# A Fourier token mixer in a four-layer network: its 32-point transforms on halves of the TensorE array, its last transform and projection by thirds of the channels

## The chip, the cores and the metric

The kernel runs on one core of one Trainium2 chip. The metric is the device time of one execution in microseconds (us). Before the change the median of three runs is 3758.2 us (3753.52 to 3759.49). One profiled execution, from which all durations below come, took 3750.98 us.

## The reference, cut to what matters

The network has four layers on an image batch of B = 4, C = 96 channels and 64 x 64 = 4096 tokens, all in float32. Layers 0 to 2 and the last feed-forward part are not touched. The change is in the first half of layer 3, which mixes tokens by a Fourier transform with H = 192 hidden channels:

```
h = relu(bn1(einsum('bnc,hc->bnh', x, w1)))
X = fft(h, axis=1, norm='ortho')
xr = relu(X.real * rd - X.imag * idg + rb)
xi = relu(X.imag * rd + X.real * idg + ib)
y = ifft(xr + 1j * xi, axis=1, norm='ortho').real
o = bn2(einsum('bnh,ch->bnc', y, w2))
t = t + o
```

Here x is the layer-normed t, and rd and idg are the diagonals of two matrices.

## The kernel before, in words

The 4096-point transform is split as 4096 = 128 x 32: a transform over 128 points, a multiplication by twiddle factors, and a transform over 32 points; the inverse goes back the same way. The 192 channels of an image are handled in groups of four, so 48 groups. A 128 x 128 matrix then holds 32 points times 4 channels in its partitions.

`fourier` runs a software pipeline of 32 iterations plus four to drain. Each iteration j starts a new set of G = 6 groups; an image takes eight iterations. The functions, with the lines of their instructions in the profile, are:

- `norm1`, `norm2` (L1306 to L1317): layer norm of the next image's tokens, in the first four iterations of each image but the last.
- `w1` (L1326, L1328): the first projection of the next image, in the other four. ScalarE writes its relu into `hh`.
- `over_n1(j)` (L1340, L1344, L1352): the 128-point transform on TensorE into `s1_ps`; VectorE multiplies it by the twiddles into `p0` and `p1`; GpSimd adds these crosswise into `f` (two instructions of 128 x 390).
- `over_n2(j-1)` (L1361 to L1364, L1367, L1376, L1379, L1380): the 32-point transform, four matmuls of 128 x 128 weights on 390 columns, into `xi_ps` and `xr_ps`; VectorE makes `ec`, ScalarE makes `av` in twelve instructions, and GpSimd adds and subtracts `ec`.
- `fold(j-2)` (L1386, L1391, L1394, L1397): a relu on ScalarE, four VectorE instructions that make `zz` and `z`, and a negation on ScalarE.
- `over_k2(j-3)` (L1409 to L1411): the inverse 32-point transform, twelve matmuls of 128 x 128 weights on 128 columns into two PSUM banks `i1`, copied by ScalarE into `bt`.
- `row64` (L1419 to L1424): the 65th row of `bt`, for which two small transfers go through DRAM.
- `over_k1` (L1444, L1446): the inverse 128-point transform for four tokens n and 96 channels (a "block"); its matrix `gt` is loaded per block by a transfer of 256 KB into one of two buffers; ScalarE copies the result to `ys`.
- `w2` (L1455, L1459, L1461): the second projection of that block, in a `misc` bank of PSUM; VectorE adds it to `t`.

A unit is half of an image's channels (96), so eight units of eight blocks, two blocks per iteration. All engines' orders are written out by hand (`manual_schedule`): each engine executes its instructions in the order of the calls. That order, within an iteration, is over_n1, norm1 or w1, fold, over_k1 of the first block, norm2, over_n2, norm1, w2 of the first block, over_k1 of the second block, over_k2, norm2 or row64 or w1, w2 of the second block. [...] `misc` two, `s1` two, `xr` and `xi` one each, `i1` two.

Of the kernel before, what the change touches and what calls it, by code (L numbers as in the profile page):

```python
# [102 lines left out]
class Net:  # L103
# [717 lines left out]
    def consts2(self, wk, small):  # L821
# [74 lines left out]
        self.a_w2 = pool.tile([C, 2, C], F32, name="a_w2s")  # L896
        for half in range(2):
            ps = small(C, C)
            nc.tensor.matmul(ps, raw[:, half * C : (half + 1) * C], gain, start=True, stop=True)
            nc.vector.tensor_copy(self.a_w2[:, half], ps)  # L900
        self.dft1 = load("dft1", [N1, 2 * 65])
        self.twid = load("twid", [128, 2, 2 * 65])
        self.dft2 = load("dft2", [128, 3 * 128])
# [381 lines left out]
    def fourier(self, dram, t, h):  # L1285
# [3 lines left out]
        units = [(b, half) for b in range(B) for half in range(2)]  # L1289
        its = [(u, g) for u in range(len(units)) for g in range(0, CG, G)]  # L1290
        with ExitStack() as ctx:
# [3 lines left out]
            nbs, bc, bs = (self.dft2[:, k * 128 : (k + 1) * 128] for k in range(3))  # L1295
# [23 lines left out]
            def w1(b, n):  # L1319

                if n == 0:
                    for half in range(2):
                        hh[2 * b + half] = wk.tile([N1, CG, N2, 4], F32, name="hh", tag="hh", bufs=3)
                ps = misc(N1)[:, : 4 * C].rearrange("p (n c) -> p n c", n=2)
                for d in range(2):
                    nc.tensor.matmul(ps[:, d, :], h[:, n + d :: N2], self.a_w1, start=True, stop=True)  # L1326
                for half in range(2):
                    nc.scalar.activation(  # L1328
                        hh[2 * b + half][:, :, n : n + 2, :].rearrange("p g n c -> p n g c"),
                        ps[:, :, half * C : (half + 1) * C].rearrange("p n (g c) -> p n g c", c=4),  # L1330
                        AF.Relu,
                    )

            def over_n1(i):

                u, g = its[i]
                ps = pln.tile([128, 2, MB], F32, name="s1_ps", tag="s1")
                for d in range(G):
                    a = d % 3 * 2 * K1
                    nc.tensor.matmul(ps[:, d // 3, a : a + 2 * K1], hh[u][:, g + d], self.dft1, start=True, stop=True)  # L1340
# [10 lines left out]
                for r in range(2):  # L1351
                    nc.gpsimd.tensor_add(f[i][:, r], pp[0][:, :, r, :], pp[1][:, :, 1 - r, :])  # L1352

            def over_n2(i):

                u, g = its[i]
                cg = units[u][1] * CG + g
                fr, fi = (f[i][:, r].rearrange("p g k -> p (g k)") for r in range(2))
                f.pop(i)
                xr, xi = (pln.tile([128, MB], F32, name=f"x{r}_ps", tag=f"x{r}")[:, : G * K1] for r in "ri")  # L1360
                nc.tensor.matmul(xi, bc, fi, start=True, stop=False)  # L1361
                nc.tensor.matmul(xi, nbs, fr, start=False, stop=True)
                nc.tensor.matmul(xr, bc, fr, start=True, stop=False)
                nc.tensor.matmul(xr, bs, fi, start=False, stop=True)  # L1364
# [17 lines left out]
            def fold(i):  # L1382

                u, g = its[i]
# [3 lines left out]
                if g == 0:  # L1388
                    z64[u] = wk.tile([128, 2, CG], F32, name="z64", tag="z64", bufs=2)
                for k, (one, two, op) in enumerate(((0, 2, ALU.add), (3, 1, ALU.subtract))):  # L1390
# [4 lines left out]
                        z64[u][:, k, g : g + G], v[:, one, :, K1 - 1], 0.0, v[:, two, :, K1 - 1], ALU.max, op  # L1395
# [3 lines left out]
            def over_k2(i):  # L1399

                u, g = its[i]
                z = zz.pop(i)
                if g == 0:
                    bt[u] = wk.tile([N1, N2, C], F32, name="bt", tag="bt", bufs=2)
                for e in range(0, G, 3):
                    ps = pln.tile([N1, 4, 128], F32, name="i1_ps", tag="i1", bufs=2)[:, :3]
                    for d in range(3):
                        zd = z[:, e + d].rearrange("p k m -> p (k m)")
                        nc.tensor.matmul(ps[:, d], zd[:, 64:], bc, start=True, stop=False)  # L1409
                        nc.tensor.matmul(ps[:, d], zd[:, :128], bs, start=False, stop=True)  # L1410
                    nc.scalar.copy(  # L1411
                        bt[u].rearrange("p n (g c) -> p g n c", c=4)[:, g + e : g + e + 3],
                        ps.rearrange("p g (n c) -> p g n c", c=4),
                    )

            def row64(u):
                ps = misc(CG)[:, :128]
                for k in range(2):
                    nc.tensor.matmul(ps, z64[u][:, k], self.dft64[:, k], start=k == 0, stop=k == 1)  # L1419
                r = wk.tile([CG, N2, 4], F32, name="r64", tag="r64", bufs=2)  # L1420
                nc.scalar.copy(r, ps.rearrange("p (n c) -> p n c", c=4))
                d = dram.tile([1, N2 * C], F32, name="d64", tag="d64", bufs=2)
# [5 lines left out]
            def fetch(k):  # L1428

                g = wk.tile([N1, CG, N2, 4], F32, name="hh", tag="hh", bufs=3)  # L1430
                g = g.rearrange("p g n c -> p (g n c)")[:, : N2 // 2 * N1].rearrange("p (n a) -> p n a", n=N2 // 2)
# [4 lines left out]
            def over_k1(u, n, kept):  # L1436
                if n in late:
                    gt = late[n]
                else:
                    gt = wk.tile([N1, 4, N1], F32, name="gt", tag="gt", bufs=2)  # L1440
                    nc.sync.dma_start(gt, ins["idft"][:, n : n + 4])
                ps = misc(C).rearrange("p (n a) -> p n a", n=4)
                for d in range(4):
                    nc.tensor.matmul(ps[:, d], bt[u][:, n + d], gt[:, d], start=True, stop=True)  # L1444
                kept[u, n] = wk.tile([C, MB], F32, name="ys", tag="ys", bufs=2)
                nc.scalar.copy(kept[u, n], ps.rearrange("p n a -> p (n a)"))  # L1446

            def w2(u, n, kept):

                b, half = units[u]  # L1450
                if u < len(units) - 1:
                    ps = misc(C)
                else:
                    ps = pln.tile([N1, 4, 128], F32, name="i1_ps", tag="i1", bufs=2)[:C].rearrange("p n a -> p (n a)")
                nc.tensor.matmul(ps, self.a_w2[:, half, :], kept.pop((u, n)), start=True, stop=True)  # L1455
                ps = ps.rearrange("p (n a) -> p n a", n=4)
                td = ft[b][:, n : n + 4]
                if half == 0:
                    nc.vector.scalar_tensor_tensor(td, ps, self.b2, td, ALU.add, ALU.add)  # L1459
                else:  # L1460
                    nc.vector.tensor_add(td, td, ps)  # L1461

            engines = {mybir.EngineType.PE, mybir.EngineType.DVE, mybir.EngineType.Activation, mybir.EngineType.Pool}
            with tc.manual_schedule(engines=engines):
# [3 lines left out]
                for j in range(len(its) + 4):  # L1468
                    ub, k = divmod(j - 2 * PER, PER)
                    blocks = [(ub, n) for n in (8 * k, 8 * k + 4)] if 0 <= ub < len(units) else []  # L1470
# [30 lines left out]
                    if blocks:  # L1501
                        w2(*blocks[0], kept)
                        over_k1(*blocks[1], kept)
# [6 lines left out]
                    if (j - 6) % PER == 0 and 0 <= (j - 6) // PER < len(units):  # L1510
                        row64((j - 6) // PER)
                    turn(len(tokens))
                    if blocks:
# [4 lines left out]
                last = [(len(units) - 1, n) for n in range(0, N2, 4)]  # L1518
# [31 lines left out]
def _constants():  # L1550
# [9 lines left out]
    th = 2 * np.pi * np.outer(np.repeat(np.arange(N2), 4), k1) / L  # L1560
# [4 lines left out]
    eye = np.eye(4)  # L1565
    bc, bs = np.kron(np.cos(th), eye), np.kron(np.sin(th), eye)
# [115 lines left out]
```

## Time and profile before

| | us |
|---|---|
| median of three runs | 3758.2 |
| profiled execution, its time | 3750.98 |
| its span, first to last instruction | 3749.2 |
| TensorE busy (share of the span) | 3115.1 (83%) |
| VectorE busy | 2981.6 (80%) |
| ScalarE busy | 2720.5 (73%) |
| GpSimd busy | 2566.7 (68%) |

The Fourier part begins at about 3108 us of the span, where its first `w1` matmul starts, and its last block ends at about 3615 us. The first matmul of `over_n1` in each iteration marks the iterations: image 0 at 3125.6 us, image 1 at 3219.1, image 2 at 3346.2, image 3 at 3470.1; the last four of an image start at 3183.9, 3281.2, 3406.9 and 3517.4 us. For images 1 and 2, an iteration is 14.7 to 16.0 us long in most cases; for image 3, where no next image is prepared, 11.6 to 12.3 us. The page's busy shares are means over the whole network; for this change one reads the rows inside 3108 to 3615 us.

In the rows, PE is TensorE's matmul, PEld its weight load, DVE VectorE, ACT ScalarE, POOL GpSimd and SP the queue that issues transfers. A float32 matmul appears as two records. A row of the timeline gives start and length in us, the engine, the line, the operation, out<-in, the shape (for TensorE: rows*columns of the weights, then the moving operand), the count, and in brackets the idle time before and who ended it.

### The profile page before, as it was taken

The page shows a single profiled execution, that of the slowest core. Times are in us where ns is not written, and L with a number is a line of the kernel's source. Part 1 is how long each engine was busy: PE and PEld are TensorE (multiplying, and loading weights), DVE is VectorE, ACT ScalarE, POOL GpSimd, SP SyncE. Part 2 cuts the span into 40 slices and gives each one's busy share as a digit, 9 for nine tenths or more (in the row PEclk, how much of TensorE's full clock was granted, in tenths as well). Part 3 has the DMA queues.
Part 4 walks back from the last instruction along what each step waited for, and adds up shares of the span by engine and source line. Part 5 has one row for each costly group of instructions (what it writes and reads, how often), then busy time and mean ns, then how long its engine had stood idle before and what let it go on. Part 6 is the DMA issues. An engine that isn't in the chain of part 4 may idle for free. (4 is left out here: it accounts for less than half of the span.)

```text
span 3749.2 us, 46836 instructions
## 1 busy us (share of the span) xinstructions
PE 3115.1 (83%) x15326; PEld 1404.9 (37%) x15326; DVE 2981.6 (80%) x2644; ACT 2720.5 (73%) x5456; POOL 2566.7 (68%) x922
## 2 busy tenths in 40 slices
PE   7887888788878887887888888657799997999888
PEld 3232223223222322232233233147344435676643
DVE  5999999999999999999999999931662493444649
ACT  6887888888888888888888888541345685656557
POOL 1899989898999899989989998811001174434527
PEclk8999899899989998999999899658899999999999
DMA  7656665666565666666665666376000000011001
GB/s 187 156 152 160 166 161 148 165 160 172 145 170 152 173 149 169 157 157 161 166 165 142 172 157 173 91 214 217 1 0 1 1 1 6 24 35 46 24 11 57
DMA packets 171644, 446.63 MB, mean 119 GB/s; under 512 B 48756, under 2 KB 50750, under 8 KB 168064
## 3 DMA queue, kind: packets, MB, share of 16 engines
q1 hardware_dynamic: 171400, 443.64, 45.7%
q8 instruction: 121, 1.98, 0.2%
q14 instruction: 123, 1.01, 0.1%
HBM read 369.97 MB, written 73.50 MB: 118 GB/s over the span
## 5 line engine op out<-in xcount | busy, mean ns | idle before, releaser
L648 POOL TENSOR_TENSOR hs<-hs,crep 128x2048 f32<-128x2048 f32 x384 | 1601.2, 4185 | 224.2 <-DVE hs L643 176.4
L610 ACT ACTIVATE da<-ddb,nega 128x1024 f32<-128x1024 f32 x576 | 661.5, 1149 | 197.7 <-DMA ddb<-dd 124.3
L643 DVE TENSOR_TENSOR_SCAN hs<-da,state,rep 128x1024 f32<-128x1024 f32 x288 | 669.2, 2338 | 39.6 <-PE rep L594 21.9
L621 POOL TENSOR_TENSOR up<-udb,brep 128x1024 f32<-128x1024 f32 x192 | 453.0, 2360 | 73.1 <-DMA udb<-ud 58.9
L665 PE MATMUL y<-hs,sel_r 128*32 128x512 f32 x3072 | 459.6, 692 | 12.8 <-POOL hs L648 12.3
L599 PE MATMUL rep<-dbl,sel_b 32*128 32x512 f32 x768 | 250.1, 730 | 215.1 <-DVE hs L643 215.0
L507 ACT ACTIVATE uta<-delta,bt 128x192 f32<-128x192 f32 x1024 | 381.1, 446 | 0.0
L287 PE MATMUL ps<-n,w_x 97*64 97x512 f32 x1536 | 353.8, 602 | 13.0 <-ACT xc L411 12.1
L643 DVE TENSOR_TENSOR_SCAN hs<-da,state,u 128x1024 f32<-128x1024 f32 x144 | 338.1, 2348 | 23.9 <-PE y L665 8.2
L643 DVE TENSOR_TENSOR_SCAN hs<-dap,state,up 128x1024 f32<-128x1024 f32 x144 | 335.2, 2328 | 0.5 <-ACT dap L610 0.5
L594 PE MATMUL rep<-ident,uta 128*128 128x128 f32 x1536 | 222.6, 287 | 105.6 <-DVE hs L643 93.2
L594 PEld LDWEIGHTS rep<-ident,uta 128*128 128x128 f32 x1536 | 174.9, 146 | 246.5 <-issue 133.3
L636 DVE TENSOR_TENSOR u<-udb,rep 128x1024 f32<-128x1024 f32 x192 | 235.4, 1226 | 24.8 <-DMA udb<-ud 11.4
L1240 POOL CAST hq<-y 128x1536 fp8e5<-128x1536 f16 x64 | 94.0, 1469 | 218.1 <-issue 122.6
L643 DVE TENSOR_TENSOR_SCAN hs<-da,rep 128x1024 f32<-128x1024 f32 x96 | 217.9, 2282 | 21.2 <-PE rep L594 14.8
L610 ACT ACTIVATE dap<-ddb,nega 128x1024 f32<-128x1024 f32 x192 | 214.8, 1119 | 24.9 <-DVE hs L643 24.4
L636 DVE TENSOR_TENSOR rep<-udb,rep 128x1024 f32<-128x1024 f32 x192 | 232.0, 1208 | 0.0
L287 PEld LDWEIGHTS ps<-n,w_x 97*64 97x64 f32 x1536 | 103.8, 137 | 260.2 <-issue 210.0
L665 PEld LDWEIGHTS y<-hs,sel_r 128*32 128x32 f32 x3072 | 73.7, 118 | 335.2 <-issue 257.7
L599 PEld LDWEIGHTS rep<-dbl,sel_b 32*128 32x128 f32 x768 | 65.8, 205 | 353.6 <-issue 295.2
L658 PE MATMUL y<-xc,dp 128*128 128x512 f32 x192 | 125.7, 743 | 31.3 <-ACT bt L463 31.3
L1379 POOL TENSOR_TENSOR av<-av,ec 128x780 f32<-128x780 f32 x32 | 58.8, 1837 | 133.7 <-ACT av L1376 133.7
(275 smaller groups left out, 6201.3 us busy)
## 6 DMA issues: line engine op xcount, KB each, us to landing
udb<-ud SPq DMA_DIRECT2D x768, 128.0 KB
ddb<-dd SPq DMA_DIRECT2D x768, 128.0 KB
crep<-cd SPq DMA_DIRECT2D x512, 128.0 KB
dd<-delta SPq DMA_DIRECT2D x64, 384.0 KB
band<-in_band SPq DMA_DIRECT2D x24, 1024.0 KB
ud<-delta SPq DMA_DIRECT2D x62, 384.0 KB
brep<-cd SPq DMA_DIRECT2D x128, 128.0 KB
x<-in_x SPq DMA_DIRECT2D x32, 384.0 KB
```

Of the source, the lines that this page charges most:

```text
L287: nc.tensor.matmul(ps[rows], w[:, 64 * p : 64 * p + 64], rhs[:, at.start + shift : at.stop + shift], start=k == 0, stop=k == len(ws) - 1, ...
L507: nc.scalar.mul(m["uta"][:, q, :, 32 * s4 : 32 * s4 + 32].rearrange("t (p j) d -> t p j d", p=3), m["udt"][:, :, q].rearrange("t p (j d) - ...
L594: nc.tensor.transpose(x[:, q * 128 : q * 128 + 128], made[k]["uta"][:, q, 2 * h + j], self.ident)
L599: nc.tensor.matmul(x[:, at], sel_b[rows, g], made[k]["dbl"][rows, at], start=True, stop=True)
L610: nc.scalar.activation(da, made[k]["dd", h, j], AF.Exp, scale=nega[:, col : col + 1])
L621: nc.gpsimd.tensor_mul(up, made[k]["ud", p][:, j], made[k]["brep", GP])
L636: nc.vector.tensor_mul(u, made[k]["ud", h][:, j], x)
L643: nc.vector.tensor_tensor_scan(hs[:, 1:], made[k].pop(("da", t)), u, st, ALU.mult, ALU.add)
L648: nc.gpsimd.tensor_mul(hs[:, :, :T], hs[:, :, 1:], twice(made[k]["crep", g]))
L658: nc.tensor.matmul(y, dp[:, items[k][2], p], made[k]["xc"][:, p], start=True, stop=True)
L665: nc.tensor.matmul(made[k]["y", p][row : row + 32], sel_r, made[k]["hs", p, g][:, j, at], start=False, stop=True, skip_group_check=True,)
L1240: nc.gpsimd.tensor_copy(q, y2, saturate=False)
```

## The change

- `over_n2`: the partitions are laid out so that real and imaginary part of two channels lie together. Four matmuls with 128 x 64 weights replace the four with 128 x 128; a pair writes the two halves of the partitions of one bank. To lay `f` out this way GpSimd makes it in four instructions of 64 x 390 instead of two of 128 x 390.
- `over_k2`: 24 matmuls with 64 rows of weights and 64 columns moving replace twelve with 128 and 128. Even and odd ones lie on the two halves of the array's rows and write two banks, `i0` and `i1`. Copies to `bt` go by bank; where a group set crosses a third of the channels there are four instead of two.
- A unit is a third of an image's channels (64), so twelve units. A block of `over_k1` is eight tokens by 64 channels: eight matmuls with 128 x 64 weights in pairs on column halves, two `gt` transfers, and one copy to `ys` of all 128 partitions. There are 48 blocks instead of 64.
- `w2`: a block's projection is two matmuls with 64 x 96 weights on row halves, into the banks `i0` and `i1` instead of a `misc` bank, and two VectorE additions to `t`.
- Schedule: units become ready after iterations 5, 8 and 10 of an image; an iteration takes one or two blocks by the pattern (2, 1, 2, 2, 1, 1, 2, 1).
- `hh`, `twid`, the small constant matrices and the vectors of `rd`, `idg`, `rb`, `ib` are laid out to fit.

```diff
-                for r in range(2):
-                    nc.gpsimd.tensor_add(f[i][:, r], pp[0][:, :, r, :], pp[1][:, :, 1 - r, :])
+                for q, rows in enumerate(parts):
+                    for r in range(2):
+                        nc.gpsimd.tensor_add(f[i][parts[r], q], pp[0][rows, :, r, :], pp[1][rows, :, 1 - r, :])
...
-                nc.tensor.matmul(xi, bc, fi, start=True, stop=False)
-                nc.tensor.matmul(xi, nbs, fr, start=False, stop=True)
-                nc.tensor.matmul(xr, bc, fr, start=True, stop=False)
-                nc.tensor.matmul(xr, bs, fi, start=False, stop=True)
+                for r, x in ((1, xi), (0, xr)):
+                    for q, rows in enumerate(parts):
+                        nc.tensor.matmul(
+                            x[rows], self.dft2[:, r], fs[:, q], start=True, stop=True, skip_group_check=True
+                        )
...
-                for e in range(0, G, 3):
-                    ps = pln.tile([N1, 4, 128], F32, name="i1_ps", tag="i1", bufs=2)[:, :3]
-                    for d in range(3):
-                        zd = z[:, e + d].rearrange("p k m -> p (k m)")
-                        nc.tensor.matmul(ps[:, d], zd[:, 64:], bc, start=True, stop=False)
-                        nc.tensor.matmul(ps[:, d], zd[:, :128], bs, start=False, stop=True)
...
+                ps = [pln.tile([N1, MB], F32, name="i_ps", tag=f"i{q}") for q in range(2)]
+                for d in range(G):
+                    zd = z[:, d].rearrange("p k m -> p (k m)")
+                    for k, m in enumerate((bc, bs)):
+                        for p, rows in zip(ps, parts):
+                            nc.tensor.matmul(
+                                p[:, d * 64 : d * 64 + 64],
+                                zd[rows, 64 - 64 * k : 192 - 64 * k],
+                                m[rows],
...
+                for d in range(4):
+                    for q, rows in enumerate(parts):
+                        nc.tensor.matmul(
+                            ps[rows, d],
+                            bt[u][:, n + 4 * q + d],
+                            gts[q][:, d],
...
-                nc.tensor.matmul(ps, self.a_w2[:, half, :], kept.pop((u, n)), start=True, stop=True)
-                ps = ps.rearrange("p (n a) -> p n a", n=4)
-                td = ft[b][:, n : n + 4]
...
+                ps = [pln.tile([N1, MB], F32, name="i_ps", tag=f"i{q}")[:C] for q in range(2)]
+                for p, rows in zip(ps, parts):
+                    nc.tensor.matmul(p, self.a_w2[rows, third], y[rows], start=True, stop=True)
+                for q, p in enumerate(ps):
+                    p = p.rearrange("p (n a) -> p n a", n=4)
+                    td = ft[b][:, n + 4 * q : n + 4 * q + 4]
...
-                    blocks = [(ub, n) for n in (8 * k, 8 * k + 4)] if 0 <= ub < len(units) else []
+                    todo += [(u, n) for r, u in ready if r + 2 == j for n in range(0, N2, 8)]
+                    many = (2, 1, 2, 2, 1, 1, 2, 1)[j % 8]
+                    blocks, todo = todo[:many], todo[many:]
...
                     if blocks:
                         w2(*blocks[0], kept)
+                    if len(blocks) > 1:
                         over_k1(*blocks[1], kept)
...
                         over_k2(j - 3)
...
-                    if blocks:
+                    if len(blocks) > 1:
                         w2(*blocks[1], kept)
```

## The prediction, before the result was known

> **What bounds the kernel now.** The page first, for the size of things, then the busy times by stretch for the Fourier part: TensorE looks like the bound.
>
> ```profile
> 3346.15:3406.86 60.71, 56.92 (x293) 36.71 (x292) 31.27 (x45) 39.60 (x95) 29.62 (x23) 1.00 0.13 36
> 3406.86:3470.05 63.19, 57.24 (x325) 46.49 (x324) 28.16 (x36) 36.80 (x107) 24.72 (x19) 1.00 0.17 51
> 3470.05:3564.50 94.45, 84.30 (x522) 63.68 (x521) 61.79 (x72) 54.22 (x146) 47.27 (x32) 1.00 0.08 24
> ```
>
> After the length come PE, PEld, DVE, ACT, POOL busy. PE fills about 90%. But a record's end lies about 0.16 us past its columns, so I read one iteration in order of time:
>
> ```profile
> 3517.43 1.50 PE L1340 MATMUL s_ps<-dft,hh 128*128 128x130 f32 x12
> 3517.63 1.25 DVE L1459 SCALAR_TENSOR_TENSOR t<-m_ps,bn_b,t 96x512 f32<-96x512 f32 x1 [3.19 <-PE m_ps L1455]
> 3519.02 1.85 DVE L1344 TENSOR_TENSOR p<-s_ps,twid 128x780 f32<-128x780 f32 x2
> 3519.43 0.85 ACT L1386 ACTIVATE av<-av 128x780 f32<-128x780 f32 x1 [2.19 <-POOL av L1380]
> 3520.79 0.55 DVE L1391 SCALAR_TENSOR_TENSOR zz<-av 128x384 f32<-128x384 f32 x1
> 3521.01 2.44 POOL L1352 TENSOR_TENSOR f<-p,p 128x390 f32<-128x390 f32 x2 [1.61 <-DVE p L1344]
> 3521.25 0.85 DVE L1394 SCALAR_TENSOR_TENSOR z<-av 128x6 f32<-128x6 f32 x1
> 3522.61 0.52 ACT L1397 ACTIVATE zz<-zz 128x384 f32<-128x384 f32 x1 [2.32 <-DVE zz L1391]
> 3523.04 0.56 ACT L1446 COPY ys<-m_ps 96x512 f32<-96x512 f32 x1
> 3523.50 3.64 ACT L1376 ACTIVATE av<-xr_ps,vec 128x65 f32<-128x65 f32 x12
> 3523.65 1.10 PE L1455 MATMUL m_ps<-ys,a_w2s 96*96 96x512 f32 x2 [1.23 <-ACT ys L1446]
> 3527.22 1.83 POOL L1379 TENSOR_TENSOR av<-av,ec 128x780 f32<-128x780 f32 x1 [3.77 <-ACT av L1376]
> 3529.01 1.50 PE L1340 MATMUL s_ps<-dft,hh 128*128 128x130 f32 x12
> 3531.02 0.86 ACT L1386 ACTIVATE av<-av 128x780 f32<-128x780 f32 x1 [2.19 <-POOL av L1380]
> ```
>
> From relu (3519.43) to relu (3531.02) is 11.59 us, a ring with no room: relu, fold on DVE, negation, ys, twelve av, two POOL operations of 1.84 us, the next relu. ACT runs in order, so av stands behind negation and ys. TensorE has slack in this ring: 1.23 us before w2. So image 3 (eight iterations, 94.5 us) is bound by the ring and not by PE. In images 1 and 2 PE and the others hand on to each other nearly without gap: with tokens, relu stands on ACT behind the second pair of hh copies, and these wait for w1. A second thing to see: z works on six elements per partition and takes 0.85 us beside f; in token iterations zz waits for f's end, and z then takes 0.16 us:
>
> ```profile
> 3460.07 1.19 DVE L1391 SCALAR_TENSOR_TENSOR zz<-av 128x384 f32<-128x384 f32 x1 [1.23 <-ACT av L1386]
> 3461.18 0.16 DVE L1394 SCALAR_TENSOR_TENSOR z<-av 128x6 f32<-128x6 f32 x1
> ```
>
> So these DVE operations, with two inputs in SBUF, wait for a running POOL operation and make the next one wait. p and ec, with one input in PSUM, keep their 0.96 us beside POOL.
>
> **The change part by part.**
>
> over_n2: 390 columns per matmul stream in 0.65 us (starts of L1361 and L1362, 3519.64 and 3520.30). L287 has 64-column weights in pairs on array halves: 1536 records of 602 ns take 353.8 us, so pairs run side by side. Four matmuls cost two: -1.31 us of PE per iteration, 42 us in all. Off the path: w2 waits for ys anyway, 1.23 us before the change, 2.5 us after.
>
> over_k2: half the rows and half the columns seem to halve it. [...] The trace says what such matmuls are paced by:
>
> ```profile
> 416.31 1.92 PE L354 MATMUL ps<-center,x 96*128 96x96 f32 x16
> 1270.38 2.82 PE L301 MATMUL ps<-xc,xproj 64*102 64x512 f32 x12
> ```
>
> L354 moves 96 columns over 128 columns of weights: 16 records in 1.92 us, 0.11 us each, as long as with 128 columns (L1409: 0.22 us per two records). The weight load sets the pace. The new matmuls load 128 columns for 64 moving ones: 24 pairs of records x 0.11 = 2.68 us, as before. I take 0. If the halves' weight loads ran one after the other it would be +2.7 us; L301, row halves at twelve records in 2.82 us, speaks for side by side.
>
> over_k1 and w2: per block unchanged on PE (0.89 and 0.86 us), 16 blocks fewer: -28 us of PE, and 16 x 0.58 = 9 us of ACT less in ys. bt copies: 80 instead of 64 of about 0.51, +4 at most.
>
> Changes of array mode: [...] The trace prices it:
>
> ```profile
> 1165.96 1.02 PE L658 MATMUL y<-xc,dp 128*128 128x512 f32 x2
> 1166.92 1.07 PE L665 MATMUL y<-hs,sel_r 128*32 128x512 f32 x8
> ```
>
> From the first start to the change is 0.96 us for two records; in one mode it is 0.87 (3528.14, an unchanged w2, to 3529.01). So 0.09 us, some seven per iteration: 0.6 us, 20 us of PE in all, mostly inside its waits.
>
> f: POOL's time goes by elements per partition (128x780 in 1.84, 128x390 in 0.93, 96x512 in 1.27 us, about 2.4 ns each), so I take 0.93 for 64x390 too: four for two, +1.9 us per iteration. By partition count it would be 0; the shift of partitions is not in the trace and could add. zz, z and f now interleave one by one, and the second zz ends 1 us (tokens) to 1.8 us (norm) later.
>
> t: two additions of 1.17 us per block, 96 for 64: +37 us of DVE. DVE has room for them (62 of 94.5 us busy); it is their place that costs. w2 now writes i0 and i1, the banks of over_k2. So over_k2, whose first two matmuls take one bank each, waits until both additions of the first block are done, and w2 of the second block waits for both bt copies. Behind these waits on PE stand norm2, w1, the next over_n1. The second block's additions stand ahead of p on DVE: 2.35 instead of 1.2 us, and behind p wait f, h and zz.
>
> gt: a block needs both buffers, so nothing is loaded ahead: about 4.1 us from issue to landing for two (one: issue 3305.64, last packet 3308.19). First to second over_k1 are 5 us apart (over_n2, the wait for ys, w2), so 0; without that cover 1 to 2 us x 20. row64's transfers (12 pairs for 8) keep two iterations of cover: 0. hh is written in single elements of 4 B: 0, at worst double, 7 us.
>
> **Sums by stage.** Image 3, one-block iteration: zz 0.55, f 0.9, z and zz 0.75, negation 0.55, ys 0.5, w2 1.05, two t 2.4, over_k2 2.7, change 0.1, over_n1 to p's start 1.6, p 1.85: 12.9 us. With two blocks, from over_k2's end: copies 1.1, w2 0.95, t 2.4 + 0.1, then p, against 1.7: +2.85, 15.8. Eight iterations have twelve blocks: 4 x 12.9 + 4 x 15.8 = 115 us against 94.5: +20.
>
> Tokens, ends counted from over_n1's start (all rows as above; hh 0.55, w1 1.82, norm 0.86, h 0.68, its square 0.63): over_n1 and w1 3.2, hh and relu 4.7, zz 7.4 (f from 3.6 or 4.6 on), negation and ys 8.4, w2 9.5, t 12.0, over_k2 14.7, w1 16.6; before, zz was at 6.4 and over_k2 followed w2 at once: 14.66. With a second w2 17.7; the first of four, whose w1 come late, 16.3. Four (blocks 1, 1, 2, 1) are 67.5 us against 64.9 and 63.2: +3.5, twice: +7.
>
> Norm, in the same way, after a one-block or a two-block iteration: p 3.4 or 4.6, h and its square 4.8 or 5.9, relu 5.5 or 6.7, zz 8.2 or 9.4, ys 9.3 or 10.5 (its copy frees the bank for norm1), norm1 and w2 11.2 or 12.4, h and t 13.7 or 14.9, over_k2 16.5 or 17.6; then bt copies and w2: 18.5 or 19.7; without a second block about 1.1 less. Four (2, 1, 2, 2) are 75 us against 62.2 and 60.7: +13.7, twice: +27.
>
> Image 0 (no blocks but one): later zz alone, 8 x 1.4: +11. Drain: 4 blocks at 2.4 us of DVE at the end for eight of 1.75 of PE, but new waits in iterations 32 to 35: 51 against 50.5, +1.
>
> Clock: a gap of 3.08 us before w2 at 3286.2 was followed by half clock:
>
> ```profile
> 3287.30:3290.70 3.40, 1.41 (x7) 0.87 (x8) 2.14 (x6) 2.45 (x8) 0.00 (x0) 1.00 0.00 0
> 3290.70:3294.10 3.40, 3.39 (x12) 2.61 (x11) 0.88 (x1) 3.10 (x11) 1.24 (x1) 0.50 0.26 77
> ```
>
> PEclk goes from 1.00 to 0.50. The new PE waits are 2 to 3 us, twice per iteration; I add six such stretches at 1.4 us: +8 (0 to 30).
>
> Sum: 20 + 7 + 27 + 11 + 1 + 8 = +74 us on the profiled 3751.0, so 3825. The median is 7.2 us above the profiled execution; for the median 3758.2 + 74 = 3832.
>
> **The rivals.**
>
> Faster, PE sets the pace: 90% busy speaks for it. Then 42 + 28 - 20 = 50 us go: 3708. It decides if over_k2 finds its banks free, that is if t ends within 1 us of w2. Against: two t take 2.35 us, and image 3's ring needs no PE. Chance 0.08.
>
> Slower, but less: DVE gets in ahead of f (-1.2 x 32 = -38) and the clock stays (-8): +28, 3786. Chance 0.14.
>
> The halves take turns at their weight loads, so the tiling doesn't do what it says: +2.7 x 32 = +86 more, 3918. Chance 0.06. Most of the wait for t would cover none of it.
>
> **How the numbers follow.** The forecast has 0.72. Around it 3795 to 3870 by the unknown terms (f 0 to +1.9, clock 0 to 30, hh 7). The range 3775 to 3890 takes in the milder rival. About 0.2% (7.5 us) is what a measurement can tell. Faster 0.08, same 0.02 (the low end of the milder case), slower 0.90.
>
> **What would show it.** Right: f four times at 0.93; over_k2 at 2.7 us; "PE i_ps <- DVE t" a long wait; w2 waiting for ys longer; image 3's iterations at 13 to 16 us; PE busy down, span up. Wrong: over_k2 at 1.4 or 5.4 us, f at half the time, image 3's iterations under 11.6 us.

## The result, and the profile after

The changed kernel takes 3879.3 us (median of four runs, 3877.7 to 3881.8) against 3755.9 for the kernel before: 1.0331 times as long, 95% interval 1.0313 to 1.0349, or +123 us. The forecast was 3832, slower, with +74 us worked out. The direction holds, and so does the range of 3775 to 3890; the result lies 9 us outside the inner 3795 to 3870 that the prediction drew from its unknown terms. The sum is 49 us short, and one of its terms, the clock, turned out to be most of that.

The page of the changed kernel: its span, the busy times, and the clock row in 40 slices (PEclk is the share of TensorE's full clock that was granted, here in tenths; the Fourier part is the seven digits before the last):

```profile
span 3876.2 us, 49184 instructions
PE 3182.6 (82%) x16438; PEld 1428.2 (37%) x16438; DVE 3034.6 (78%) x2677; ACT 2730.9 (70%) x5460; POOL 2638.3 (68%) x986
PEclk8899998999999899999999987589999988887779
```

PE was to do 50 us less and is 67 us busier than before (3115.1). Now the Fourier part by stages: image 0; norm and token iterations of image 1; the same of image 2; seven iterations of image 3; the rest to the last addition to t. After the length come PE, PEld, DVE, ACT and POOL busy, then PEclk:

```profile
3128.54:3233.69 105.15, 84.19 (x513) 59.73 (x513) 46.38 (x57) 63.94 (x167) 69.28 (x54) 0.84 0.02 6
3233.69:3313.79 80.10, 66.01 (x452) 38.31 (x453) 40.88 (x49) 40.22 (x98) 40.11 (x31) 0.87 0.16 47
3313.79:3390.32 76.53, 61.30 (x441) 48.51 (x439) 35.83 (x40) 39.74 (x106) 34.16 (x26) 0.82 0.12 36
3390.32:3475.97 85.65, 72.53 (x453) 42.59 (x453) 40.78 (x49) 40.26 (x98) 40.09 (x31) 0.80 0.15 44
3475.97:3553.93 77.96, 62.83 (x442) 49.08 (x440) 35.82 (x40) 39.88 (x106) 34.14 (x26) 0.79 0.16 48
3553.93:3667.66 113.73, 88.70 (x708) 64.51 (x708) 59.45 (x70) 47.59 (x132) 55.47 (x42) 0.80 0.10 29
3667.66:3742.30 74.64, 60.40 (x469) 40.03 (x468) 36.68 (x42) 22.38 (x54) 11.60 (x8) 0.77 0.01 1
```

The same seven stages of the kernel before took 93.4, 62.2, 64.9, 60.7, 63.2, 82.8 and 63.3 us, at a clock of 0.95 to 1.00. Every stage has grown, and in every stage PE has lost 13 to 23% of its clock. One iteration of image 3 in order of time (rows of the timeline, as in the prediction):

```profile
3633.31 2.97 PE L1351 MATMUL s_ps<-dft,hh 128*128 128x130 f32 x12
...
3637.26 0.82 PE L1373 MATMUL xi_ps<-f,dft 128*64 128x390 f32 x4
...
3638.36 4.46 POOL L1364 TENSOR_TENSOR f<-p,p 64x390 f32<-64x390 f32 x4 [6.27 <-DVE p L1355]
...
3639.95 0.52 ACT L1408 ACTIVATE zz<-zz 128x384 f32<-128x384 f32 x1 [5.30 <-DVE zz L1402]
3640.38 0.57 ACT L1479 COPY ys<-m_ps 128x512 f32<-128x512 f32 x1
...
3641.00 1.10 PE L1487 MATMUL i_ps<-ys,a_w2s 64*96 64x512 f32 x4 [2.26 <-ACT ys L1479]
3642.13 2.16 DVE L1494 TENSOR_TENSOR t<-t,i_ps 96x512 f32<-96x512 f32 x2 [0.43 <-PE i_ps L1487]
...
3643.33 0.69 PE L1419 MATMUL i_ps<-idft,zz 64*128 64x64 f32 x2 [1.22 <-DVE t L1494]
...
3644.35 5.38 PE L1419 MATMUL i_ps<-idft,zz 64*128 64x64 f32 x46 [0.33 <-DVE t L1494]
...
3650.62 2.97 PE L1351 MATMUL s_ps<-dft,hh 128*128 128x130 f32 x12
```

The waits that the prediction named are there: w2 waits 2.26 us for ys, over_k2's first pair 1.22 us for t. The iteration is 17.3 us long; the seven of image 3 take 15.0 to 17.3, where the prediction had 13 to 16. But over_n1 takes 2.97 us instead of 1.50, and over_k2 5.38 us for 46 of its 48 records. That is half clock: PEclk is 0.50 over each of the two. In image 0, at full clock (PEclk 1.00) and with no wait inside, all of over_k2 is one row of this trace:

```profile
3162.93 2.90 PE L1419 MATMUL i_ps<-idft,zz 64*128 64x64 f32 x48
```

The kernel before takes 2.84 us for it, from its first start to its last end. Over the part as a whole (groups of f and hh before the change; f, hh and over_k2 after it; with the idle time before them):

```profile
L1352 POOL TENSOR_TENSOR f<-p,p 128x390 f32<-128x390 f32 x64 | 65.2, 1039 | 97.2 <-DVE p L1344 94.5 <-PE m_ps L1444 2.7
L1328 ACT ACTIVATE hh<-m_ps 128x192 f32<-128x192 f32 x128 | 35.3, 337 | 41.3 <-PE m_ps L1326 41.1
```

```profile
L1364 POOL TENSOR_TENSOR f<-p,p 64x390 f32<-64x390 f32 x128 | 137.2, 1072 | 184.7 <-DVE p L1355 168.6 <-PE xr_ps L1373 5.0 <-PE m_ps L1336 4.5
L1338 ACT ACTIVATE hh<-m_ps 128x192 f32<-128x192 f32 x128 | 53.3, 530 | 40.8 <-PE m_ps L1336 40.5
L1419 PE MATMUL i_ps<-idft,zz 64*128 64x64 f32 x1536 | 139.5, 334 | 28.7 <-DVE t L1492 16.0 <-DVE t L1494 12.6
```

f on 64 partitions costs per instruction what it cost on 128 (1072 ns; before 1039): four for two, as forecast. hh written in single elements takes 530 ns instead of 337. over_k2's matmuls wait for t for 28.7 us in all.

### The profile page after: what moved, and what is told of

It is laid out like the page before. It is cut to its first block, busy times and chain, and to the rows that moved or that the text cites. A ratio compares the mean times of both kernels' runs of the same rounds, so it can differ in the third digit from the quotient of the medians.

```text
span 3876.2 us, 49184 instructions
## 1 busy us (share of the span) xinstructions
PE 3182.6 (82%) x16438; PEld 1428.2 (37%) x16438; DVE 3034.6 (78%) x2677; ACT 2730.9 (70%) x5460; POOL 2638.3 (68%) x986
## 3 DMA queue, kind: packets, MB, share of 16 engines
q14 instruction: 124, 1.02, 0.1%
## 5 line engine op out<-in xcount | busy, mean ns | idle before, releaser
L1364 POOL TENSOR_TENSOR f<-p,p 64x390 f32<-64x390 f32 x128 | 137.2, 1072 | 184.7 <-DVE p L1355 168.6
L1355 DVE TENSOR_TENSOR p<-s_ps,twid 128x780 f32<-128x780 f32 x64 | 59.0, 962 | 172.0 <-issue 138.1
```

The lines of the kernel that those rows point to most:

```text
L1364: nc.gpsimd.tensor_add(f[i][parts[r], q], pp[0][rows, :, r, :], pp[1][rows, :, 1 - r, :])
```

## The experiments

A name that begins with `a_` is the changed kernel with an edit, one with `b_` the kernel before with an edit; `fill` is a group of matmuls whose result nobody reads. Each ratio is against runs of the kernel before on the same chip. The chips differ from row to row (the kernel before takes 3748 to 3756 us on them), so a difference between two rows is given from the medians and, where it matters, from the ratios. "Stages" is the time from image 0's first matmul to the last addition to t; "half clock" is worked out from the stage rows of each trace, twice (1 - PEclk) times the length, summed over the seven stages. These two columns come from one profiled execution, which in some rows lies up to 10 us from the median (a_fill 3819, a_fill_whole 3808).

| kernel | us | ratio, 95% interval | stages, us | half clock, us |
|---|---|---|---|---|
| before (profile of the prediction) | | 1 | 490.6 | 22 |
| changed | 3879.3 | 1.0331 (1.0313 to 1.0349) | 613.8 | 229 |
| b_shared | 3749.8 | 0.9996 (0.9987 to 1.0004) | 494.3 | 41 |
| a_misc | 3892.3 | 1.0377 (1.0361 to 1.0393) | 629.1 | 297 |
| a_whole | 3851.1 | 1.0269 (1.0247 to 1.0290) | 591.1 | 189 |
| a_fill | 3810.1 | 1.0162 (1.0142 to 1.0182) | 556.0 | 24 |
| b_thirds | 3762.6 | 1.0031 (1.0019 to 1.0043) | 501.5 | 26 |
| b_fwd | 3788.2 | 1.0100 (1.0084 to 1.0115) | 529.4 | 106 |
| a_fill_whole | 3817.5 | 1.0182 (1.0165 to 1.0199) | 549.6 | 53 |
| a_fill_hhrun | 3823.9 | 1.0197 (1.0182 to 1.0212) | 564.9 | 52 |
| a_k2whole | 3794.0 | 1.0113 (1.0095 to 1.0131) | 535.6 | 98 |
| a_k2inter | 3794.7 | 1.0120 (1.0103 to 1.0137) | 543.1 | 98 |
| b_fill8 | 3744.6 | 0.9985 (0.9978 to 0.9992) | 488.2 | 15 |
| b_thirds_best | 3762.9 | 1.0030 (1.0020 to 1.0040) | 508.8 | 27 |

**Is it the shared banks?** First the price of sharing by itself, in the kernel before:

```diff
-                if u < len(units) - 1:
+                if False:
                     ps = misc(C)
```

> The kernel before with one edit: w2 always writes an i1 buffer (over_k2's), not m_ps; one addition of t per block of four tokens as before. It is the price of sharing the banks alone, with one bank and one addition instead of two. Theory: the first half of over_k2 finds the other buffer free only once bt's copy is done, the second half waits for t (1.2 us after w2, of which the first half covers 1.3): +5 to +25 us, 3761 to 3781. Rival (m_ps is the tighter ring, so w2 elsewhere helps norm and over_k1): -5 to -15 us. If sharing alone costs over 60 us, the changed kernel's second addition is not what matters.

No difference. The second kernel gives w2 other banks in the changed kernel:

```diff
-                ps = [pln.tile([N1, MB], F32, name="i_ps", tag=f"i{q}")[:C] for q in range(2)]
+                ps = [misc(C) for _ in range(2)]
```

> The changed kernel with one edit: w2's two products go to two m_ps banks instead of to i0 and i1, the banks of over_k2. Theory (over_k2 stands behind both additions of t because it shares their banks; this wait and the half clock that follows it are the largest part of the +123 us): PE's waits on DVE t at L1419 (about 75 us in the changed kernel) go, the granted clock of the Fourier stage rises from 0.8 to about 0.9, 50 us are won: 3830. Rival 1 (the ring relu, zz, f on DVE and GpSimd sets the length; PE's wait only fills the time that the ring takes anyway): 0 to 10 us, 3870 to 3880. Rival 2 (the wait only moves: the next user of an m_ps bank, over_k1, norm or w1, then waits for t): no gain or slower, 3875 to 3900.

It is 13 us slower than the changed kernel (17 by the ratios): rival 2. (The wait of about 75 us in the text above adds PE's 28.7 us to those of PEld, the weight loads, which lie over the same time.) A token iteration of it, from the timeline:

```profile
3355.89 1.10 PE L1487 MATMUL m_ps<-ys,a_w2s 64*96 64x512 f32 x4 [2.49 <-ACT ys L1479]
3357.03 2.19 DVE L1494 TENSOR_TENSOR t<-t,m_ps 96x512 f32<-96x512 f32 x2 [0.43 <-PE m_ps L1487]
...
3358.22 1.90 PE L1470 MATMUL m_ps<-gt,bt 128*64 128x128 f32 x16 [1.23 <-DVE t L1494]
...
3360.06 1.33 PE L1419 MATMUL i_ps<-idft,zz 64*128 64x64 f32 x10
```

over_k2 waits for nothing here. The next block's over_k1, which stands ahead of it and wants an m_ps bank too, waits the same 1.23 us for t. The wait has moved to the next user of the bank, and in token iterations the clock is down to 0.70 and 0.67.

**Is it f? Is it the clock?** The forward transform is put back on the whole array:

```diff
-                for q, rows in enumerate(parts):
-                    for r in range(2):
-                        nc.gpsimd.tensor_add(f[i][parts[r], q], pp[0][rows, :, r, :], pp[1][rows, :, 1 - r, :])
+                for r in range(2):
+                    nc.gpsimd.tensor_add(f[i][:, r], pp[0][:, :, r, :], pp[1][:, :, 1 - r, :])
```

> The changed kernel with the forward 32-point transform put back on the whole array: f as two GpSimd additions of 128x390 instead of four of 64x390, over_n2 as four matmuls with 128 columns. Everything else as changed. Theory (four f of 0.93 us each hold up zz on DVE by 1 to 1.8 us in each of 32 iterations): 32 x 1.4 = 45 us come back, 3834, although PE gets 42 us more to do, all of it in the wait for ys. Rival (the wait for t at over_k2 sets the length, zz has waited there anyway): within 8 us of the changed kernel. Rival 2 (PE's work counts because PE at half clock is the bound): slower, up to 42 us, 3920.

28 us come back (23 by the ratios), of the 45 expected; and 40 us of half clock go at the same time, so this run alone doesn't part f from the clock. Filling PE's waits does:

```diff
+            def fill(count):
+                ps = pln.tile([128, 2, MB], F32, name="s1_ps", tag="s1")
+                for _ in range(count):
+                    nc.tensor.matmul(ps[:, 0, : 2 * K1], self.ident, self.dft1, start=True, stop=True)
...
+                    if j < len(its):
+                        fill(7)
                     if blocks:
                         w2(*blocks[0], kept)
...
+                    if j < len(its):
+                        fill(4)
                     if 3 <= j < len(its) + 3:
                         over_k2(j - 3)
```

> The changed kernel with matmuls added whose result nobody reads: seven of 128x130 (0.2 us each at full clock) after over_n2, in the wait for ys, and four before over_k2, in the wait for t. They write the s1 bank, which is free there. Theory (the half clock that the new gaps bring is a term of its own, some 45 to 50 us of the +123): granted clock of the Fourier stage from 0.8 to over 0.93, over_k2 2.6 us throughout, 25 to 45 us won, 3835 to 3855. Rival (half clock only lengthens work that lies in waits): clock up, time within 10 us of 3879. Rival 2 (the fillings push PE beyond its waits): slower, up to 32 x 0.8 = 26 us, 3905.

352 matmuls more, and 69 us less (63 by the ratios). The stage rows of this kernel (PEclk is the third number from the end):

```profile
3127.31:3229.89 102.58, 93.50 (x689) 71.41 (x689) 47.02 (x57) 64.10 (x167) 69.24 (x54) 0.98 0.02 6
3229.89:3306.94 77.05, 66.68 (x540) 42.81 (x541) 40.99 (x49) 40.17 (x98) 40.13 (x31) 1.00 0.17 49
3306.94:3373.44 66.50, 61.48 (x530) 50.03 (x528) 35.41 (x40) 39.52 (x106) 34.17 (x26) 1.00 0.13 41
3517.04:3615.06 98.02, 91.66 (x862) 69.81 (x862) 58.08 (x70) 47.22 (x132) 56.08 (x42) 0.97 0.11 34
```

DVE, ACT and POOL do the same work in the same busy time; what has changed, beside the fillings themselves, is the clock. So the clock is a term of its own: 58 us of the stages (613.8 - 556.0) in this execution, which was the slowest of four, against 65 that remain. It can be more, because the fillings can also hold PE up.

**The two parts by themselves.** b_thirds is the kernel before with thirds, eight-token blocks, w2 in i0 and i1 and two additions of t (the changed code of over_k1, w2 and the schedule); b_fwd is the kernel before with f and over_n2 on halves and the layout of hh that goes with them. Both keep over_k2 on the whole array.

> The second part of the change alone: thirds of the channels, blocks of eight tokens side by side, w2's pair in i0 and i1, two additions of t. hh's layout, f, over_n2 and over_k2 are those of the kernel before. Theory (with the clock held by fillings the changed kernel lost about 60 us, of which image 0 with f and hh alone lost 1.1 us per iteration; so t and the banks make 60 - 32 x 1.1 = 25 us, and their gaps make 30 to 40 us of half clock): 3805 to 3815, granted clock of the Fourier stage near 0.85. Rival 1 (f's longer way is what turns t's additions into waits; without it they lie beside other work): within 10 us of 3750. Rival 2 (28 us of PE saved come through): 3720 to 3740.

> The first part of the change alone: hh with its channels ahead of its tokens, f as four GpSimd additions of 64x390, over_n2 on halves; over_k2 on the whole array, over_k1, w2 and t as in the kernel before. Theory (zz 1.1 us later in each of 32 iterations, and PE's longer waits bring some half clock): +35 from zz, +5 to +25 from the clock, 3790 to 3810; w2 goes on waiting for ys only. Rival 1 (the whole loss needs t's waits): within 10 us of 3750. Rival 2 (42 us of PE saved come through): 3710 to 3740.

b_thirds costs 12 us, nearly rival 1: its norm, token and image 3 rows are

```profile
3226.38:3291.11 64.73, 58.80 (x356) 34.87 (x357) 35.01 (x49) 39.85 (x97) 30.14 (x23) 1.00 0.20 58
3291.11:3351.06 59.95, 54.52 (x346) 42.31 (x344) 31.94 (x40) 35.55 (x105) 25.34 (x18) 1.00 0.15 45
3475.72:3563.77 88.05, 77.09 (x540) 52.95 (x540) 58.65 (x70) 47.43 (x129) 42.52 (x28) 1.00 0.12 37
```

In these rows the clock stays whole (it is 0.91 in image 0, which is 7 us longer than before, and 0.94 at the end). Token stages are 3 to 5 us shorter than before, where PE's saving shows; norm stages and image 3 lose 2.5 to 5 us each. b_fwd costs 37 us, just under its theory's 3790 to 3810, with image 3's row at a clock of 0.91 and 106 us of half clock in all. Together that makes 49 of the 123 us. Neither part holds the rest; what both leave out is over_k2 on halves.

**f and hh with the clock held.** Two kernels with fillings; the first has f and over_n2 on the whole array (and two fillings where the other had seven), the second writes hh in runs:

```diff
-                        hh[2 * b + half][:, :, :, n : n + 2].rearrange("p g c n -> p n (g c)"),
-                        ps[:, :, half * C : (half + 1) * C],
+                        hh[2 * b + half][:, :, n : n + 2, :].rearrange("p g n c -> p n g c"),
+                        ps[:, :, half * C : (half + 1) * C].rearrange("p n (g c) -> p n g c", c=4),
```

> The changed kernel with fillings that nobody reads (two instead of seven matmuls of 128x130 before w2, four before over_k2) and with f and over_n2 put back on the whole array: what f costs once the clock is held. Theory (f's ring and the clock are terms of their own): 3810 - 37 = 3773, image 0 near 94 us, clock over 0.95. Rival (without half clock f's delay lies beside other work; the 28 us that it won in the kernel without fillings were clock): 3800 to 3815.

> The changed kernel with fillings (seven and four) and with hh written in runs of four channels (16 B) as in the kernel before; the transforms after it take the elements in the other order, so its output is of permuted tokens and channels. What ScalarE's single 4-byte writes cost. hh measured 527 ns instead of 331 in the changed kernel: 128 x 0.2 = 25 us of ScalarE. Theory (most of it lies beside other work; the prediction bounded it by 0 and 7 us): 0 to -7 us, 3803 to 3810. Rival (hh stands ahead of relu and so of zz in token iterations, and in the w1 run ahead of image 0 nothing covers it): -12 to -25 us, 3785 to 3798.

The first is the rival's case: 3817 against 3810, no gain. (In the profiled executions its stages are 1 to 3 us shorter than a_fill's, except in image 3; but that execution was the fastest of its four and a_fill's the slowest, so these differences show nothing.) So in the changed kernel, with the clock held for the most part (53 us of half clock are left), f's longer way costs nothing that can be seen; yet alone in the kernel before (b_fwd) f and its layout cost 37 us. How much of the 37 is clock was not tried. The second is 14 us slower than a_fill, which neither theory had; ScalarE's own time fell as expected (token stage 35.2 us instead of 39.5), the token stage stayed at 66.3, and what grew (image 3, 103.8 us, and one norm stage, 80.0) lies where the clock was 0.91 instead of 0.97, and 0.94 instead of 1.00; why it was lower there is not known. The single-element writes cost ScalarE 18 us (53.3 us busy against 35.3) and the kernel nothing that these runs can see.

**over_k2 on the whole array.** This is the run that finds the rest:

```diff
-                for d in range(G):
-                    zd = z[:, d].rearrange("p k m -> p (k m)")
-                    for k, m in enumerate((bc, bs)):
-                        for p, rows in zip(ps, parts):
-                            nc.tensor.matmul(
-                                p[:, d * 64 : d * 64 + 64],
-                                zd[rows, 64 - 64 * k : 192 - 64 * k],
-                                m[rows],
-                                start=k == 0,
-                                stop=k == 1,
-                            )
+                for q in range(2):
+                    ps = pln.tile([N1, MB], F32, name="i_ps", tag=f"i{q}")[:, :384].rearrange("p (g k) -> p g k", g=3)
+                    for d in range(3):
+                        zd = z[:, 3 * q + d].rearrange("p k m -> p (k m)")
+                        nc.tensor.matmul(ps[:, d], zd[:, 64:], bc, start=True, stop=False)
+                        nc.tensor.matmul(ps[:, d], zd[:, :128], bs, start=False, stop=True)
```

> The changed kernel with over_k2 put back on the whole array: four matmuls of 128 rows for each pair of channel groups, the first three groups in i0, the other three in i1, bt copied bank by bank; everything else as changed. PE's own time for it is the same, 2.6 us. New theory (each half of over_k2 keeps a bank of its own, so its first pair wants both banks, after both additions of t, and both banks end only with its last pair; on the whole array the first bank starts after one addition and its copy lies beside the second half; the half clock then fed on the gaps): the two parts alone cost 12 and 37 us, so 3762 + 37 = 3800, or up to 3815 with some half clock of both. Rival (the prediction's figure: halves here cost nothing): 3870 to 3880. Rival 2 (the parts' gaps add up to half clock even so): 3840 to 3860.

3794: of the 123 us, 80 to 85 are tied to over_k2's halves, an edit that by itself leaves PE's time at full clock where it was. Its stages (four norm, four token, seven image 3 iterations) have a clock of 0.98 and 0.88 where the changed kernel's had 0.79 and 0.80:

```profile
3363.56:3432.07 68.51, 55.77 (x357) 31.40 (x358) 41.03 (x49) 40.10 (x97) 40.15 (x31) 0.98 0.19 55
3432.07:3500.89 68.82, 55.88 (x346) 44.81 (x344) 35.29 (x40) 40.00 (x105) 34.16 (x26) 0.88 0.18 54
3500.89:3597.14 96.25, 76.18 (x541) 53.63 (x541) 56.98 (x70) 48.24 (x130) 56.23 (x42) 0.88 0.12 34
```

My explanation at that point was the banks: on halves, the first pair of matmuls wants both banks, and both end only with the last pair. That has a test of its own, the same whole-array matmuls in an order that ties the banks together in the same way:

```diff
-                for q in range(2):
-                    ps = ...
-                    for d in range(3):
+                for d in range(3):
+                    for q, ps in enumerate(pair):
                         zd = z[:, 3 * q + d].rearrange("p k m -> p (k m)")
```

> The kernel with over_k2 on the whole array (3794), with only the order of its 24 matmuls changed: after each channel group of bank i0 comes one of bank i1, so that over_k2 wants both banks within its first 0.3 us and completes both only at its end, as the halves of the changed kernel do. Same matmuls, same banks, same copies. Theory (what over_k2 on halves costs, 85 us, is the two banks tied together and the half clock that follows): most of the 85 us comes back, 3850 to 3880, granted clock of the Fourier stage near 0.82. Rival (it is the halves as such, their weight loads, twice the records and the changes of array mode): 3794, within 10 us. In between, 3815 to 3840: both.

3794.7. The banks' theory falls; it is the halves as such. Which property of them, the two kernels can only suggest. This iteration of a_k2whole has the same waits as the one of the changed kernel above: 2.4 us before w2, then 1.23 us for t. Its clock is at half already in w2 (2.02 us for four records, where the changed kernel's took 1.10), and over_k2 starts at half clock as it did there (PE rows of the timeline; each L1418 or L1419 row is one matmul of 128 columns):

```profile
3563.03 2.02 PE L1482 MATMUL i_ps<-ys,a_w2s 64*96 64x512 f32 x4 [2.39 <-ACT ys L1474]
3566.28 0.80 PE L1418 MATMUL i_ps<-idft,zz 128*128 128x128 f32 x2 [1.23 <-DVE t L1489]
3566.87 0.64 PE L1419 MATMUL i_ps<-idft,zz 128*128 128x128 f32 x2
3567.29 0.63 PE L1418 MATMUL i_ps<-idft,zz 128*128 128x128 f32 x2
...
3569.43 0.47 PE L1419 MATMUL i_ps<-idft,zz 128*128 128x128 f32 x2
3569.74 0.39 PE L1418 MATMUL i_ps<-idft,zz 128*128 128x128 f32 x2
...
3570.63 1.50 PE L1351 MATMUL s_ps<-dft,hh 128*128 128x130 f32 x12
```

At about 3569.6 us the clock is back: matmuls follow at 0.22 us instead of 0.43, and over_n1 takes 1.50 us. In the changed kernel over_k2 went through its 5.38 us at half clock and over_n1 after it too. In the seven stages the clock record of a_k2inter has 21 stretches of half clock, 4.6 us long on average; that of the changed kernel 29, and 7.9 us long: it falls more often, and above all it stays down longer. The wait for t (PE, over_k2) is 16 us in a_k2whole, 22 us in a_k2inter and 28.7 us in the changed kernel; the first two have 98 us of half clock each, so the waits explain little of the 131 us more.

What differs is how much moves through the array. At half clock the whole-array matmuls pass 128 columns in 0.43 us. On halves, 46 records are 23 matmuls in pairs, 64 columns for each pair: 11.5 x 64 = 736 columns in 5.38 us, or 59 in 0.43 us, half as many. PEld is busy 5.19 of these 5.38 us, so I read the weight loads as what sets the pace. Here 5.38 us of gapless records did not bring the clock back, and whole-array matmuls did. The other half clock of the changed kernel's seven stages agrees. Its 29 stretches are 3.4 to 17.1 us long by the clock record. In the last 3.41 us of each (the length of the shortest), ahead of full clock, records filled 100% of the time (median). What lies before that, ahead of more half clock, makes 38 pieces of the same length, and records filled 99% of those (median). By an estimate from 0.87 us for two records of 512 columns at full clock and twice that at half, with pairs of halves counted once, the 38 pieces moved columns for 50% of their time and the 29 for 89% (medians; the two kinds overlap a little near 80%). That the clock comes back with the columns moved is the reading that fits; the runs show that it stays down longer with over_k2 on halves (229 us of half clock against the 98 of a_k2whole), not why.

Two things were not tried: over_k2 on halves alone in the kernel before, and the fillings in a_k2whole. a_fill, with halves and the clock held, is still 16 us slower than a_k2whole, which has 98 us of half clock; whether that is the halves' own or the fillings' is open.

**A version that beats both.** Two tries, one from each side. b_fill8 puts `fill(5)` ahead of w2's place for j < 8 into the kernel before; b_thirds_best puts it into b_thirds, and changes the pattern of blocks:

```diff
-                    many = (2, 1, 2, 2, 1, 1, 2, 1)[j % 8]
+                    many = (1, 1, 1, 2, 2, 1, 2, 2)[j % 8]
```

> The kernel before with fillings that nobody reads: five matmuls of 128x130 before w2's place in the eight iterations of image 0, where its granted clock was 0.96. Theory (half clock costs here too): image 0 from 93.4 to 90 us, -3 to -6 us, 3745 to 3748. Rival (the eight iterations are bound by ScalarE and GpSimd at full clock as well, and the fillings only take PE's time): 0 to +6 us.

> A try for a version that beats both: thirds and blocks of eight tokens on the forward half and over_k2 of the kernel before (3763 by itself), with the same five fillings in image 0, and with the blocks moved from norm iterations (5 instead of 7 of each image) to token iterations (7 instead of 5), which had gained. Theory: image 0 -5, norm iterations 2 x -2 us, 3753, the same as before. Rival 1 (a second block costs in token iterations what it cost in norm ones): 3758. Rival 2 (token iterations have the room, norm ones win over 1 us per block): 3745, faster than before.

b_fill8 is 0.15% faster than the kernel before, the only version that is; but not where I expected it: image 0 stays at 94.1 us and a clock of 0.96, and the 3 us that the profile shows are in image 1, at a clock of 1.00 instead of 0.96. The fillings stand in image 0's iterations alone; what they have to do with image 1 is not shown. b_thirds_best gains 2.7 us in each norm stage, loses 4.3 in each token stage, and image 3 takes 91.8 us instead of 88.0: nearest to rival 1's 3758, and no better than b_thirds.

## Why the prediction was right, and what was mis-sized

- **over_k2 takes as long on halves as before: right on PE, wrong in what it costs.** 2.90 us at full clock against 2.84 (2.6 from the first start to the last in both), as the weight loads had it; half the rows and half the columns did not halve it. "I take 0" was the step that failed: putting only over_k2 back on the whole array returns 80 to 85 us, and 131 us of half clock go with it. The prediction's sign of being wrong, over_k2 at 5.4 us, does appear (5.38 us), but in iterations at half clock, not because the halves take turns.
- **The clock, +8 (0 to 30): the mis-sized term.** It is 58 to 69 us by the run with fillings. The prediction had seen that a gap of 3.08 us is followed by half clock and counted six such stretches of 3.4 us, with no reason for six; there were 29, and they lasted 7.9 us on average. "PE busy down" failed with it: PE's records last longer at half clock (over_n1 2.97 us instead of 1.50), and its busy time rose by 67 us.
- **The sum without the clock, 66 us: 65 in the stages of a_fill, partly by luck.** By stages image 0 was to be 104.5 and is 102.6, norm 75 and 77.1, tokens 67.5 and 66.5, image 3 with the drain 166 and 166.2. But fillings may hold PE up, that profiled execution was 9 us above its median, and the causes under the sum are less sure: b_thirds, whose f is the old one, has 100.3 us in image 0, so "later zz alone" need not be what makes that stage longer, and f on the whole array (a_fill_whole) won nothing. (The four token entries add up to 67.2, not 67.5.)
- **f, four at 0.93 us instead of two: right in the instruction** (1072 ns against 1039, waits for DVE included), and 37 us when done alone, where 32 x 1.2 is 38. That they agree may be luck: b_fwd has 84 us more half clock than the kernel before, which the 38 did not hold. In the changed kernel its removal gave 23 to 28 us, while 40 us of half clock went, and nothing with the clock held.
- **t and the banks.** The wait of PE on t is there and the second part's order of events too, but alone (b_thirds) it costs 12 us, not 28; and one bank shared with one addition costs nothing (b_shared). Taking the banks apart only moved the wait.
- **over_n2's and over_k1's pairs run side by side: right** (at full clock, 0.82 us per two matmuls of 390 columns, 1.09 per eight of 128), and no gain from it shows in images 0 and 3 of any run. In token stages b_thirds is 3 to 5 us shorter, with less for PE to do.
- **hh, 0 to 7, a bound that was an estimate without a row under it: not contradicted.** The writes take 1.6 times as long (530 ns against 337) and keep ScalarE busy for 18 us more, and a_fill_hhrun, without them, won nothing; but it was 14 us slower for a reason that stays open. Changes of array mode, gt and row64: no row shows a cost.
- **The rivals.** "PE sets the pace" is out: +123 instead of -50. The milder one supposed that the clock stays; in b_thirds it nearly does, in the changed kernel it does not. Weight loads in turn: out, over_k2 is 2.90 us at full clock. What was missing is a rival in which the halves do what they say and the clock answers.

## What to carry to other kernels

Before TensorE is given fewer columns to move in a stage where it already waits, look at the granted clock and at what will bring it back after each wait: here whole-array matmuls did, about 3.3 us after their start (a_k2whole), and 5.38 us of halves did not. To tell a clock term from a wait, fill the waits with matmuls that nobody reads; here the kernel got 69 us faster while half clock went from 229 to 24 us (a_fill), so it was the clock. And price the parts of a change alone: here two of them cost 12 and 37 us alone and 41 to 47 together (a_k2whole, a_k2inter), and the third, which looked free, cost 80 to 85 beside them. A bank taken out of one wait gave the wait, 1.23 us, to its next user (a_misc).

## What the runs showed of the hardware that I had not expected

- At half clock, 46 half-array matmul records of 64 columns in 5.38 us left the clock at half in the iteration shown; in that of a_k2whole, whole-array ones of 128 columns had it back about 3.3 us after their start.
- Weight loads slow down with the clock too: 46 of over_k2's took 5.19 us at half clock, and 48 took 2.76 us at full clock (image 0 of the changed kernel).
- ScalarE's relu from PSUM to SBUF with 192 elements per partition takes 337 ns when four written elements lie together and 530 ns when each lies by itself.
- A GpSimd addition on 64 partitions takes as long as on 128 (1072 and 1039 ns on average), as the prediction took it. No cost shows for moving the result to the other 64 partitions: of f's first two the second moves it, and they take 0.88 and 1.02 us (medians), where the two before the change took 0.89 and 1.03.
